# A two-layer diffusion transformer: the total of the softmax sums formed between two key products, two scalings put later, the first loads on two queues, and the second feed-forward network's first elements placed anew

## The chip, the cores and the metric

The kernel runs on one core of one Trainium2 chip. A core has TensorE (matmuls, with weight loads that overlap them), VectorE, ScalarE, GpSimd and SyncE (which here only issues transfers); ScalarE can issue transfers as well. The metric is the device time of one execution in microseconds, with the median over several runs. Lower is better.

## The reference

Sixteen images of 256 tokens with 256 features go through two blocks. Each block is self-attention, cross-attention to a context of 256 tokens with 192 features, and a feed-forward network; every part starts with a layer norm whose scale and shift come from a conditioning vector. All is float32.

```python
# layer 0: 16 heads of 64, rotary positions, inner width 1024
attn_in = adaln(x, cond, ln1, g1, b1)
x = attn(attn_in, attn_in, sa_wq, sa_wkv, sa_wo, sa_bo) + x
x = attn(adaln(x, cond, ln1, g1, b1), ln(context), ca_wq, ca_wkv, ca_wo, ca_bo) + x
x = gelu(adaln(x, cond, ln2, g2, b2) @ ff_w1 + ff_b1) @ ff_w2 + ff_b2 + x
# layer 1: 16 heads of 16, six modulations from silu(cond) @ Wmod + bmod
x = x + attn(h1 @ Wqkv + bqkv) @ Wos + bos
x = x + attn(h2 @ Wq + bq, context @ Wk + bk, context @ Wv + bv) @ Woc + boc
x = x + gelu(h3 @ W1 + b1) @ W2 + b2
# attn: rope(q), rope(k) in layer 0; softmax(q k^T / sqrt(width of a head)) v
```

## The kernel before, in words

**Order.** The kernel writes out the order of work on every engine by hand: a manual schedule covers TensorE (PE), VectorE (DVE), ScalarE (ACT), GpSimd (POOL) and SyncE (SP), and each engine runs its instructions in the order in which the code issues them. Where a line of the code stands is therefore where its instruction stands in its engine's queue. Transfers that SP issues go out in that order too, and one whose data isn't ready holds back those behind it.

**Phases, jobs, steps.** There are six phases: layer 0's self-attention, cross-attention and feed-forward network (phases 0, 1, 2), and layer 1's (3, 4, 5). A phase has 16 jobs, one for each image `b`. A job of attention has two steps (`s` = 0, 1), a job of a feed-forward network four. A job is called by phase and image: 5_2 is image 2 in the last phase. A loop runs over all steps, and each step ends with `scores(i + 1)`, the 128 score matmuls of the next attention step (L751) with their exponentials on ACT (L764, four of 128x1024 a step). So a step of attention stretches from one scores run to the next; the one that forms the probabilities, the sums and the outputs of one half of the heads also prepares queries, keys and values for what follows. PSUM is eight banks of 512 float32 a partition, placed by number; scores fill all eight, four for each half `u` of the step.

**Layer 0's self-attention.** For a step, `stage_t` (L770, DVE) adds the probabilities over pairs of keys, `stage_turn` (L776) transposes the result in 32x32 blocks, and `stage_reduce` (L783) sums it. When a job's four halves are there, `sum_up` forms the totals with one small product against a constant `fold` (eight short matmuls "banks<-fold,rows", L84), takes the reciprocal (L792), writes it to DRAM (`sums_seen`, L795) and reads it back spread over partitions (`spread`, L798, four transfers). `scale` (L807, POOL) multiplies the raw outputs by it, one call for each of four parts. `keys(then, e, half)` forms the keys of the next step, `rotate` the rotary products m (L613 for queries, L619 for keys, DVE) and their differences and sums qk (L628, POOL), which the next scores read. `layer0_sums` forms the probability-weighted values (L818).

Two products are done by a seven-product scheme in place of eight. For the queries this holds in the steps of images 3 to 15 (`queries_by_seven`), for the values it holds for images 2 to 15 (`by_seven`). Where both hold in the first step of a job, the code sets `seven`: these are the first steps of images 3 to 14, twelve in all. `late` is the job before, whose totals are formed there, and `nxt` the one after, whose values are. In them `value_part` forms the next image's values in seven products (L643 to L660 are its copies and additions); its "join" (L654, DVE) adds bank 4 to a part of v, and frees that bank for the last part.

**The next images.** `moments` (L352 to L358) finds the statistics of x, `prepare_norm` the normalized x (L366) and its blockwise transposition (L376, `blocks`), which goes on through DRAM: SP writes `turned` (L381) and reads `fetched` (L391). From `fetched` come the scaled and shifted transposed inputs hT (L424 and L426 on ACT, L428 on POOL or DVE). Images ahead go through this some steps early.

**The start.** SP issues, in this order, the condition, x of image 0, `rows` (all the vectors, 34 KB), the first half of wk and wq, the rotary table, the two halves of wv, x of images 1 and 2, `fold`, `mask`, the second half of wk and wq, bo, wo, and x of images 3 to 15. ACT issues the two modulation matrices (`mod_a`). PE turns `rows` into columns (L156, copied by L157), forms the modulation (L188, L196), transposes the normalized x of image 0 (L1254) and then makes the first products with hT (L84, from 11.06 us). It does some idle products with the identity (L140) between these.

**Feed-forward networks.** Each has also a seven-product form. From a few input blocks `fold_input` (L936 to L939, DVE) forms combinations of hT, called `inner`; `fold_output_weights` (L1010 to L1013, DVE, four operations of 128x512) does the same for the second matrix. In the last phase, images 0 and 1 pass their steps with ordinary products (`ffn_products`, ACT's L903 reads them) while the weights and the inputs of images 2 and 3 are folded; from there on L969 and L989 (DVE) add up pieces of the seven products. Banks of the ordinary products go round by a counter, `next_bank()`.

```python
    def next_bank():
        turn_of_ffn[0] = (turn_of_ffn[0] + 1) % 8
        return turn_of_ffn[0]
```

Of the kernel before, what the change touches and what calls it, by code (L numbers as in the profile page):

```python
# [10 lines left out]
F32 = mybir.dt.float32  # L11
# [32 lines left out]
def fast(ctx: ExitStack, tc: tile.TileContext, a: dict, out: bass.AP, flag):  # L44
# [99 lines left out]
    def condition():  # L144

        sig = work.tile([NB, D], F32, tag="inv", name="sig")
        nc.scalar.activation(sig, cond, AF.Sigmoid)
        soon = stat.tile([NB, 1], F32, tag="ve", name="soon")
# [126 lines left out]
    def load_layer0_attention(kind, part, between=None):  # L275
# [3 lines left out]
        if part in ("first", "last"):  # L279
            i = ("first", "last").index(part)  # L280
            wk, wq = (wtile([P, 2, 512], f"w{n}{i}", f"w{n}{i}_{kind}") for n in "kq")
            nc.sync.dma_start(out=wk, in_=wkv_src[:, :, halves[i]])
            nc.sync.dma_start(out=wq, in_=chunked(a[f"{kind}_wq"])[:, :, halves[i]])
            w[f"wk{i}"], w[f"wq{i}"] = wk, wq
            if between is not None and i == 0:
                between()
# [74 lines left out]
    def normalized(src, found, width, name):  # L361

        mv, rstd = found
        xh = work.tile([P, NT, width], F32, tag="xh", name=f"xh_{name}", bufs=1)
# [798 lines left out]
    def count_outside():  # L1163
# [9 lines left out]
        {"layer": 0, "kind": "attn", "cross": False, "load": lambda part: load_layer0_attention("sa", part, load_first),  # L1173
# [9 lines left out]

    def load_first():

        nc.sync.dma_start(out=rope, in_=a["rope"])
        load_phase(0, "values")
        for b in range(1, 3):
            load_x(b)
        for dst, name in ((fold, "fold"), (mask, "mask")):  # L1190
            nc.sync.dma_start(out=dst, in_=a[name])
# [43 lines left out]
    phases[0]["make_mod"] = phases[0]["mod_load"]()  # L1235
    load_x(0)
    nc.sync.dma_start(out=rows, in_=a["rows"])
    for part in ("first", "last", "early", "output"):
        load_phase(0, part)
    for b in range(3, NB):  # L1240
        load_x(b)

    silu = condition()
    jobs[0]["hraw"] = banks[:, 6:8, 0:N]
    found = moments(xs[0], "first")
    xh = normalized(xs[0], found, D, "first")  # L1250
    phases[0]["mod"] = phases[0]["make_mod"](3, silu)
    for c in range(KC):
        for t in range(NT):
            nc.tensor.transpose(  # L1254
                jobs[0]["hraw"][:, c, t * P : (t + 1) * P], xh[:, t, c * P : (c + 1) * P], ident
            )
    idle_products(2)
# [14 lines left out]
    for i, (j, s) in enumerate(steps):  # L1272
# [39 lines left out]
        if ffn:  # L1312
# [8 lines left out]
            if b == 0 and s == (1 if layer0 else 0):  # L1321
# [36 lines left out]
            if s == 2:  # L1358
# [5 lines left out]
                if b == 1:  # L1364
                    fold_output_weights(job["phase"], nc.vector)
                    if not layer0:
# [6 lines left out]
            if s == 3:  # L1373
# [23 lines left out]
                elif b == 1:  # L1397
                    fold_input(jobs[j + 1 : j + 3], nc.vector)
                    prepare_moments(fourth)
        elif layer0:  # L1400
# [10 lines left out]
            if queries_by_seven(then):  # L1411
# [3 lines left out]
                stage_t(job, 2 * s)  # L1415
                stage_turn(job, 2 * s)
# [778 lines left out]
```

## Time and profile before

| | |
|---|---|
| median of three runs | 2155.43 us (2154.51 to 2158.4) |
| the profiled execution | 2155.3 us, with a span of 2153.5 us |
| PE busy | 2134.9 us (99%) |
| DVE busy | 1665.5 us (77%) |
| POOL busy | 1338.1 us (62%) |
| ACT busy | 905.2 us (42%) |
| DMA | 117.83 MB, 55 GB/s on average |
| granted clock of PE | 9 of 9 tenths shown, in every slice of the span |

The span runs from the first to the last instruction that the profiler recorded; the execution's own time is 1.8 us longer. Matmuls are pipelined and their ends are modelled, so a busy PE is not a PE at its peak. A group in the timeline shows its start, its busy time, the engine, the line, the output and inputs, how many instructions it holds, and in brackets the idle time before it with what ended it. In the rows of groups the busy time, the mean of one in ns, and the idle time with its releaser follow each other. "DMA a<-b" as a releaser means that the transfer into a had to land.

### The profile page before, as it was taken

The page shows a single profiled execution, that of the slowest core. Times are in us where ns is not written, and L with a number is a line of the kernel's source. Part 1 is how long each engine was busy: PE and PEld are TensorE (multiplying, and loading weights), DVE is VectorE, ACT ScalarE, POOL GpSimd, SP SyncE. Part 2 cuts the span into 40 slices and gives each one's busy share as a digit, 9 for nine tenths or more (in the row PEclk, how much of TensorE's full clock was granted, in tenths as well). Part 3 has the DMA queues.
Part 4 walks back from the last instruction along what each step waited for, and adds up shares of the span by engine and source line. Part 5 has one row for each costly group of instructions (what it writes and reads, how often), then busy time and mean ns, then how long its engine had stood idle before and what let it go on. Part 6 is the DMA issues. An engine that isn't in the chain of part 4 may idle for free.

```text
span 2153.5 us, 112523 instructions
## 1 busy us (share of the span) xinstructions
PE 2134.9 (99%) x51248; PEld 1440.9 (67%) x51248; DVE 1665.5 (77%) x3060; ACT 905.2 (42%) x1455; POOL 1338.1 (62%) x1346
## 2 busy tenths in 40 slices
PE   9999999999999999999999999999999999999998
PEld 5666767766766666666666668887655656566787
DVE  6877887877888988888888777864777777777765
ACT  3333333333333332333323334443666666665442
POOL 4888778778767877686776766672322323235773
PEclk9999999999999999999999999999999999999999
DMA  6111110110133221211212123221221232223321
GB/s 196 30 38 23 28 38 23 29 38 23 32 87 88 76 59 35 60 42 44 59 35 59 26 73 94 54 48 23 63 44 41 48 102 63 57 49 82 75 64 39
DMA packets 307039, 117.83 MB, mean 55 GB/s; under 512 B 243364, under 2 KB 289784, under 8 KB 306424
## 3 DMA queue, kind: packets, MB, share of 16 engines
q1 hardware_dynamic: 306008, 110.02, 20.5%
q8 instruction: 403, 6.60, 1.3%
q14 instruction: 84, 0.69, 0.1%
q10 hardware_dynamic: 544, 0.52, 0.1%
HBM read 77.14 MB, written 33.29 MB: 51 GB/s over the span
## 4 chain that ended last, share of the span: by engine, by line
PE 66%; POOL 2%; DVE 1%; SPq 0%; DMA 0%; issue 0%; ACT 0%; DVEq 0%; POOLq 0%; ACTq 0%
PE banks L84 42%; PE banks L751 11%; PE banks L837 5%; PE banks L818 5%; PE banks L687 1%; PE banks L504 1%; POOL raw L807 1%; POOL qk L716 0%; POOL folded L1100 0%; DMA spread<-sums_seen 0%; DVE x L1054 0%; POOL folded L1023 0%; SPq L381 0%; SPq L391 0%; SPq L798 0%
## 5 line engine op out<-in xcount | busy, mean ns | idle before, releaser
L764 ACT ACTIVATE pr<-banks 128x1024 f32<-128x1024 f32 x576 | 487.3, 937 | 442.9 <-PE banks L751 312.6
L716 POOL TENSOR_TENSOR qk<-m,m 128x512 f32<-128x512 f32 x152 | 222.3, 1484 | 121.4 <-DVE m L708 118.6
L751 PE MATMUL banks<-qk 32*64 32x256 f32 x8192 | 242.1, 378 | 5.2 <-POOL qk L628 4.3
L770 DVE TENSOR_TENSOR both<-pr 128x1024 f32<-128x1024 f32 x128 | 168.9, 1319 | 94.5 <-ACT pr L764 92.7
L818 PE MATMUL banks<-pr,v 128*32 128x256 f32 x4096 | 240.5, 379 | 0.0
L751 PEld LDWEIGHTS banks<-qk 32*64 32x64 f32 x8192 | 183.8, 131 | 68.1 <-POOL qk L628 18.5
L828 ACT COPY raw<-banks 128x512 f32<-128x512 f32 x128 | 75.1, 587 | 331.1 <-PE banks L818 300.4
L708 DVE TENSOR_TENSOR m<-banks,rope 128x512 f32<-128x512 f32 x304 | 189.6, 678 | 18.5 <-POOL qk L716 10.9
L628 POOL TENSOR_TENSOR qk<-m,m 128x256 f32<-128x256 f32 x208 | 166.1, 824 | 57.9 <-DVE m L619 33.0
L818 PEld LDWEIGHTS banks<-pr,v 128*32 128x32 f32 x4096 | 132.4, 110 | 93.5 <-issue 16.8
L807 POOL TENSOR_TENSOR raw<-raw,spread 128x512 f32<-128x512 f32 x128 | 162.3, 1298 | 36.2 <-DMA spread<-sums_seen 34.7
L454 POOL TENSOR_TENSOR x<-x,bo_b 128x256 f32<-128x256 f32 x96 | 73.3, 783 | 163.5 <-DVE xh L366 163.5
L879 POOL TENSOR_TENSOR oT<-oT,spread 128x256 f32<-128x256 f32 x64 | 45.8, 737 | 205.5 <-DVE spread L878 205.5
L776 DVE STREAM_TRANSPOSE squares<-both 128x1024 f32<-128x1024 f32 x128 | 158.7, 1240 | 2.2
L783 DVE TENSOR_REDUCE rows<-squares 128x32 f32<-128x1024 f32 x128 | 155.0, 1211 | 1.3
L1100 POOL TENSOR_TENSOR folded<-raw,raw 128x512 f32<-128x512 f32 x90 | 143.1, 1617 | 2.4
L837 PE MATMUL banks<-pr,wide_v 128*32 128x256 f32 x2048 | 134.3, 379 | 0.0
L84 PE MATMUL banks<-hT,wq_ca 128*32 128x256 f32 x2048 | 133.9, 379 | 0.0
L751 PE MATMUL banks<-q,k 32*64 32x256 f32 x4096 | 127.9, 381 | 0.0
L84 PE MATMUL banks<-hT,wk_sa 128*32 128x256 f32 x2048 | 125.2, 381 | 0.5 <-ACT hT L424 0.5
L1054 DVE TENSOR_TENSOR x<-banks,x 128x256 f32<-128x256 f32 (+2 forms) x150 | 79.6, 531 | 55.4 <-PE banks L84 49.0
L751 PEld LDWEIGHTS banks<-q,k 32*64 32x64 f32 x4096 | 87.5, 131 | 37.7 <-issue 13.6
(270 smaller groups left out, 4392.1 us busy)
## 6 DMA issues: line engine op xcount, KB each, us to landing
turned<-blocks SPq DMA_DIRECT2D x380, 64.0 KB
fetched<-turned SPq DMA_DIRECT2D x380, 64.0 KB
spread<-sums_seen SPq DMA_DIRECT2D x128, 128.0 KB
x<-in_x SPq DMA_DIRECT2D x16, 256.0 KB
fetched_c<-turned_c SPq DMA_DIRECT2D x64, 64.0 KB
cT<-in_ctx_turned SPq DMA_DIRECT2D x16, 256.0 KB
out<-x SPq DMA_DIRECT2D x15, 256.0 KB
ctx<-in_ctx SPq DMA_DIRECT2D x16, 192.0 KB
```

The costliest lines, as they stand in the source:

```text
L84: nc.tensor.matmul(out[cut], lhsT[:, cut], rhs, start=start, stop=stop, **more)
L628: nc.gpsimd.tensor_tensor(out, cos[i], sin[1 - i], (ALU.subtract, ALU.add)[i])
L708: nc.vector.tensor_tensor(m, pq, rope[:, s : s + 1, :].to_broadcast([P, 2, N]), ALU.mult)
L716: nc.gpsimd.tensor_tensor(r, x, y, (ALU.subtract, ALU.add)[out])
L751: nc.tensor.matmul(banks[64 * g : 64 * g + 64, at + h, t * N : (t + 1) * N], lhs, rhs, start=(half == 0 and (t == 0 or job["layer"] == 1)) ...
L764: nc.scalar.activation(pr[:, one], sc[:, one], AF.Exp, scale=0.125 if job["layer"] == 0 else 0.25)
L770: nc.vector.tensor_tensor(both, pr[:, :, 0, :], pr[:, :, 1, :], ALU.add)
L776: nc.vector.transpose(job["squares"].rearrange("p b k -> p (b k)"), job.pop("both").rearrange("p h n -> p (h n)"))
L783: nc.vector.tensor_reduce(job["rows"][:, u, :], job.pop("squares"), AX.X, ALU.add)
L807: nc.gpsimd.tensor_tensor(part, part, spread[:, u : u + 1, :].to_broadcast([P, 2, N]), ALU.mult)
L818: nc.tensor.matmul(o[32 * h : 32 * h + 32, half, :], v[:, t, col : col + 32], pr[:, h, t, :], start=(t == 0), stop=(t == NT - 1),)
L837: nc.tensor.matmul(o[32 * h : 32 * h + 32], v[:, t, 4 * c + h, 32 * e : 32 * e + 32], pr[:, h, t, :], start=(t == 0), stop=(t == NT - 1),)
```

## The change

Nothing is added to what is computed, and no shapes change. Four things are placed differently.

- **Start.** `rows` goes out second on SP, ahead of x of image 0, and `fold` and `mask` follow x. The first half of wk, wq and the rotary table are issued by ACT, between the sigmoid of the condition and the exponential of the condition (`soon`). The normalized x of image 0 lies in a buffer of the weights' pool that wv uses later, and the loads of wv and all behind it stand after the four transposes of that x in the code.
- **The twelve `seven` steps.** The total is formed in bank 3 between the two halves of the first keys, with its reciprocal and transfers there; before, it was formed in bank 5 after the first part of the values. `scale` is called for parts 0 and 1 where it was called for 0, 1 and 2, and for 2 and 3 at the end, where it was called for 3. The "join" stands ahead of the first half of `layer0_sums`.
- **The border to layer 1's feed-forward network.** In the last step of its cross-attention, the normalization of image 2 and the moments of image 3 for the network are issued between the two halves of the sums (they stood after both, and in the next step). The counter of banks is set to 7, so that the first step's own products begin with bank 0.
- **The folding of the second matrix** in layer 1's feed-forward network stands in the last step of image 1, behind `fold_input`, and no longer in the step before.

```diff
@@ -141,10 +141,11 @@
                 bank(0, 2, P), ident, ident.unsqueeze(1).to_broadcast([P, 2, P]), start=True, stop=True
             )
-    def condition():
+    def condition(load):
         sig = work.tile([NB, D], F32, tag="inv", name="sig")
         nc.scalar.activation(sig, cond, AF.Sigmoid)
+        load()
         soon = stat.tile([NB, 1], F32, tag="ve", name="soon")
         nc.scalar.activation(soon, cond[:, 0:1], AF.Exp)
         silu = work.tile([NB, D], F32, tag="inv", name="silu")
@@ -272,18 +273,16 @@
-    def load_layer0_attention(kind, part, between=None):
+    def load_layer0_attention(kind, part, eng=nc.sync):
         halves = [slice(i * 512, (i + 1) * 512) for i in range(4)]
         wkv_src = chunked(a[f"{kind}_wkv"])
         w = {}
         if part in ("first", "last"):
             i = ("first", "last").index(part)
             wk, wq = (wtile([P, 2, 512], f"w{n}{i}", f"w{n}{i}_{kind}") for n in "kq")
-            nc.sync.dma_start(out=wk, in_=wkv_src[:, :, halves[i]])
-            nc.sync.dma_start(out=wq, in_=chunked(a[f"{kind}_wq"])[:, :, halves[i]])
+            eng.dma_start(out=wk, in_=wkv_src[:, :, halves[i]])
+            eng.dma_start(out=wq, in_=chunked(a[f"{kind}_wq"])[:, :, halves[i]])
             w[f"wk{i}"], w[f"wq{i}"] = wk, wq
-            if between is not None and i == 0:
-                between()
         if part == "values":
             w["wv"] = wtile([P, 2, H * 64], "wv", f"wv_{kind}")
             for i in range(2):
@@ -358,10 +357,10 @@
         nc.gpsimd.tensor_tensor(rstd, ve, neg_half, ALU.pow)
         return mv, rstd
-    def normalized(src, found, width, name):
+    def normalized(src, found, width, name, pool=work, tag="xh"):
         mv, rstd = found
-        xh = work.tile([P, NT, width], F32, tag="xh", name=f"xh_{name}", bufs=1)
+        xh = pool.tile([P, NT, width], F32, tag=tag, name=f"xh_{name}", bufs=1)
         for t in range(NT):
             nc.vector.tensor_scalar(
                 xh[:, t, :], src[:, t, :], mv[:, t, 0:1], rstd[:, t : t + 1], ALU.subtract, ALU.mult
@@ -1170,7 +1169,7 @@
     phases = [
-        {"layer": 0, "kind": "attn", "cross": False, "load": lambda part: load_layer0_attention("sa", part, load_first),
+        {"layer": 0, "kind": "attn", "cross": False, "load": lambda part: load_layer0_attention("sa", part, nc.scalar if part == "first" else nc.sync),
          "mod_load": lambda: layer0_modulation(1)},
         {"layer": 0, "kind": "attn", "cross": True, "load": lambda part: load_layer0_attention("ca", part), "mod_load": None},
         {"layer": 0, "kind": "ffn", "cross": False, "mod_load": lambda: layer0_modulation(2),
@@ -1180,15 +1179,6 @@
         {"layer": 1, "kind": "ffn", "cross": False, "mod_load": lambda: layer1_modulation(3),
          "load": lambda part: load_ffn("L1_xcond_W1", "L1_xcond_W2", "L1_xcond_b1", "L1_xcond_b2", "b", part)},
     ]
-    def load_first():
-        nc.sync.dma_start(out=rope, in_=a["rope"])
-        load_phase(0, "values")
-        for b in range(1, 3):
-            load_x(b)
-        for dst, name in ((fold, "fold"), (mask, "mask")):
-            nc.sync.dma_start(out=dst, in_=a[name])
     def load_phase(p, part):
         ph = phases[p]
@@ -1233,27 +1223,33 @@
             stage_rotary(then[0], 2 * then[1] + e, half, 2 * e)
     phases[0]["make_mod"] = phases[0]["mod_load"]()
+    nc.sync.dma_start(out=rows, in_=a["rows"])
     load_x(0)
-    nc.sync.dma_start(out=rows, in_=a["rows"])
-    for part in ("first", "last", "early", "output"):
-        load_phase(0, part)
-    for b in range(3, NB):
-        load_x(b)
-    silu = condition()
+    for dst, name in ((fold, "fold"), (mask, "mask")):
+        nc.sync.dma_start(out=dst, in_=a[name])
+    def load_first():
+        load_phase(0, "first")
+        nc.scalar.dma_start(out=rope, in_=a["rope"])
+    silu = condition(load_first)
     jobs[0]["hraw"] = banks[:, 6:8, 0:N]
     found = moments(xs[0], "first")
-    xh = normalized(xs[0], found, D, "first")
+    xh = normalized(xs[0], found, D, "first", wpool, "wv")
     phases[0]["mod"] = phases[0]["make_mod"](3, silu)
     for c in range(KC):
         for t in range(NT):
             nc.tensor.transpose(
                 jobs[0]["hraw"][:, c, t * P : (t + 1) * P], xh[:, t, c * P : (c + 1) * P], ident
             )
+    load_phase(0, "values")
+    for b in range(1, 3):
+        load_x(b)
+    for part in ("last", "early", "output"):
+        load_phase(0, part)
+    for b in range(3, NB):
+        load_x(b)
     idle_products(2)
     prepare_input(jobs[0])
     for e in range(2):
@@ -1318,7 +1314,9 @@
             fourth = jobs[j + 4] if j + 4 < len(jobs) and b < NB - 1 else None
             if s == 1 and b > 0 and third is not None:
                 prepare_norm(third)
-            if b == 0 and s == (1 if layer0 else 0):
+            if b == 0 and s == 0 and not layer0:
+                turn_of_ffn[0] = 7
+            if b == 0 and s == 1 and layer0:
                 prepare_moments(third)
             if b == 2 and s == 0 and layer0:
                 add = finish(jobs[j - 3], next_bank(), later=True)
@@ -1362,8 +1360,9 @@
                     prepare_norm(third)
                     prepare_fetch(after)
                 if b == 1:
-                    fold_output_weights(job["phase"], nc.vector)
-                    if not layer0:
+                    if layer0:
+                        fold_output_weights(job["phase"], nc.vector)
+                    else:
                         show_sums(jobs[j - 2])
                         for one in jobs[j + 1 : j + 3]:
                             prepare_input(one, nc.scalar)
@@ -1396,6 +1395,8 @@
                     scale(prev)
                 elif b == 1:
                     fold_input(jobs[j + 1 : j + 3], nc.vector)
+                    if not layer0:
+                        fold_output_weights(job["phase"], nc.vector)
                     prepare_moments(fourth)
         elif layer0:
             then = attention(i + 1, 0)
@@ -1413,17 +1414,19 @@
                 if seven:
                     fold_tokens(nxt, nc.gpsimd)
                 stage_t(job, 2 * s)
+                keys(then, 0, 0)
+                if seven:
+                    sum_up(late, 3)
                 stage_turn(job, 2 * s)
-                for half in range(2):
-                    keys(then, 0, half)
+                keys(then, 0, 1)
                 rotate(then, 0, 1)
                 query_part(then, 0)
                 if s == 1:
                     fold_inner(late, nc.gpsimd, 7, 6)
                 if seven:
                     value_part(nxt, 0)
-                if s == 0:
-                    sum_up(late, 5 if seven else 6)
+                elif s == 0:
+                    sum_up(late, 6)
                 if make_mod:
                     make_mod["mod"] = make_mod["make_mod"](6)
                 for half in range(2):
@@ -1433,7 +1436,7 @@
                 stage_reduce(job, 2 * s)
                 if seven:
                     rotate(then, 1, 1)
-                    scale(late, 0, 1, 2)
+                    scale(late, 0, 1)
                     value_part(nxt, 1)
                     query_part(then, 2)
                     query_part(then, 3)
@@ -1441,17 +1444,17 @@
                     value_part(nxt, "first")
                     query_part(then, 4)
                     value_part(nxt, 2)
+                    value_part(nxt, "join")
                     layer0_sums(job, 0, 5, (0,))
                     query_part(then, 5)
                     rotate(then, 0, 0)
                     query_part(then, 6)
                     rotate(then, 1, 0)
                     layer0_sums(job, 0, 5, (1,))
-                    value_part(nxt, "join")
                     value_part(nxt, 3)
                     layer0_sums(job, 1, 6)
                     value_part(nxt, 4)
-                    scale(late, 3)
+                    scale(late, 2, 3)
                 else:
                     query_part(then, 2)
                     layer0_sums(job, 2 * s, 4)
@@ -1551,8 +1554,12 @@
                 stage_a(then[0], then[1], at)
             if nxt["kind"] == "ffn" and s == 1:
                 ffn_products(nxt, 0, at)
+            border = nxt["kind"] == "ffn" and s == 1
             for e in range(2):
                 layer1_sums(job, s, e, at + 2 + e)
+                if border and e == 0:
+                    prepare_norm(third)
+                    prepare_moments(jobs[j + 4])
                 if s == 1:
                     finish(prev, at + 1, (e,))
                 elif nxt["kind"] == "attn":
@@ -1564,7 +1571,8 @@
             if s == 0:
                 prepare_moments(third)
             else:
-                prepare_norm(third)
+                if not border:
+                    prepare_norm(third)
                 prepare_input(after)
                 if job["cross"] and job["b"] == 5:
                     fold_input_weights(phases[job["p"] + 1], nc.gpsimd)
```

## The prediction

> **What bounds the kernel now.** I read the page first: busy rows, then the chain of waits.
>
> ```profile
> PE 2134.9 (99%) x51248; PEld 1440.9 (67%) x51248; DVE 1665.5 (77%) x3060; ACT 905.2 (42%) x1455; POOL 1338.1 (62%) x1346
> ...
> PE 66%; POOL 2%; DVE 1%; SPq 0%; DMA 0%; issue 0%; ACT 0%; DVEq 0%; POOLq 0%; ACTq 0%
> ...
> L751 PE MATMUL banks<-qk 32*64 32x256 f32 x8192 | 242.1, 378 | 5.2 <-POOL qk L628 4.3
> ...
> L751 PEld LDWEIGHTS banks<-qk 32*64 32x64 f32 x8192 | 183.8, 131 | 68.1 <-POOL qk L628 18.5
> ...
> L807 POOL TENSOR_TENSOR raw<-raw,spread 128x512 f32<-128x512 f32 x128 | 162.3, 1298 | 36.2 <-DMA spread<-sums_seen 34.7
> ```
>
> TensorE is busy 99% and holds the chain, so work moved on VectorE, GpSimd or a queue pays only where TensorE waits for it. The last three rows name one such wait: layer 0's self scores (L751) wait for the rotated pair (L628, GpSimd), and GpSimd waits for the spread reciprocals (L807). The page doesn't say in which steps; the timeline does. From one scores run to the next, the steps that form the next image's values by seven products take 19.93 us at their best (starts 182.58, 222.36, 262.15) and 20.31 to 21.10 at worst. Here is the worst, 585.92 to 607.02:
>
> ```profile
> 594.27 0.36 DVE L792 RECIPROCAL inv<-banks 128x32 f32<-128x32 f32 x1 [0.64 <-ACT banks L643]
> ...
> 602.51 3.77 POOL L807 TENSOR_TENSOR raw<-raw,spread 128x512 f32<-128x512 f32 x3 [2.92 <-DMA spread<-sums_seen]
> ...
> 604.85 0.16 PEld L84 LDWEIGHTS banks<-sums_of_weights,hT 128*32 128x32 f32 x8 [0.39 <-DVE v L654]
> ...
> 606.23 2.11 POOL L628 TENSOR_TENSOR qk<-m,m 128x256 f32<-128x256 f32 x3
> ...
> 607.02 1.35 PE L751 MATMUL banks<-qk 32*64 32x256 f32 x28 [1.10 <-POOL qk L628]
> ```
>
> GpSimd idles 2.92 us until the spread lands, does three scalings (3.77), and only then the rotary pairs which the scores need: TensorE waits 1.10. The 0.39 is a second wait: the fifth value product waits for the join (L654), queued behind four rotary operations.
>
> **Seven steps** (twelve: images 3 to 14, first half). The total's matmul moves between the two first key products, the reciprocal ahead of the turn (L776) and the rotaries, two of four scalings go behind the rotary pairs, the join ahead of L613. No operation is added.
>
> Stalls at the end of these steps, beyond the steady 0.28 us of TensorE between two scores runs, read step by step: 0.55, 0.39, 0.55, 0.61, 0.01, 0.90, 0.65, 1.17, none in three others: 4.83 us. The eight steps behind them take 20.11 us in place of 19.85, where the scores' second half waits 0.206 for the last pair: 1.65. Together 6.48. (The twelfth step, from 141.85, waits 0.73 for the folded tokens, L532, which the change leaves.)
>
> What becomes of them, in the clean step from 262.15: TensorE reaches the total at 265.79 plus half of 1.93, 266.75. VectorE ends L770 at 267.40, so the reciprocal runs there, and no longer at 270.50: 3.1 us earlier. The spread, whose wait ended at 277.07, is there at about 274, when GpSimd has just begun a rotary pair (274.40 to 275.83). Then two scalings, 2 x 1.26, to 278.4; the rotary pairs, which could start when VectorE's products are there (278.7 and 280.4), end at 281.8, before 282.08. Two scalings follow (2.6 us) ahead of L1100, which took 4.83 from 284.92 after a scaling that ended at 284.85; they now end at about 284.7, so nothing behind them is late. Seven of the eight stalls go. In the worst step SP holds the reciprocal: four issues of turned_c (591.04 to 594.91) and ctx (to 595.57) precede it, so its transfer leaves at 595.67 as before; only the scaling order helps, 1.3 of GpSimd time against a stall of 1.4, and 0.3 remains. So -6.2. The join now fits VectorE's idle 1.68 us ahead of L613 (601.18); the wait it causes is of size 0.1 (TensorE) in the clean steps, twelve times: -1.2. Sum -7.4. Bounds: -8 if the worst step is cured too; -5 if two more stalls of 0.6 stay, and half of the second waits and joins (1.2 + 0.8 + 0.6 less).
>
> The new wait: the total's bank is one that the second Exp (L764) of the step reads. Four take 3.77 from 264.20, so the second ends at 266.09, 0.66 ahead of TensorE. Counted at nothing under that cover.
>
> **The start.** TensorE's first product of x waits for this chain:
>
> ```profile
> 1.65 0.41 SPq L1237 DMA_DIRECT2D rows<-in_rows  x1
> ...
> 5.30 0.37 PE L156 MATMUL banks<-ident,rows 68*128 68x68 f32 x1 [0.98 <-DMA rows<-in_rows]
> ...
> 11.06 1.07 PE L84 MATMUL banks<-hT,wk_sa 128*32 128x256 f32 x16 [0.53 <-ACT hT L424]
> ```
>
> rows goes out second, not third. TensorE's idle products end at 4.31, so its transpose runs 0.98 earlier at best; x's load goes out 0.46 later, and the statistics (L352, 5.85, with x landed at 4.86) gain 0.5 to 1.0. The first product comes at about 10.0 to 10.5. wk, wq and rope move to ScalarE's queue behind its sigmoid (3.00, 0.42): issued at about 3.45 rather than 2.10, wk has 6.5 us to land where it took 7.15 (landed 9.25) among the same bytes; wq is needed 0.67 later. They hold ScalarE's table load (3.44) by 1.3 us; its next work is at 8.56, so that is covered. Against it: wv's load now waits for the transposes of x (L1254, 9.05 to 9.67; the tile shares its buffer) and leaves at about 8.9, not 3.55, with x1 to x15 behind it. The loads run at some 380 GB/s (8 to 28 us), so the stream's end moves by 0 to 0.8; at its end stands image 1's turned input, whose hT (L424, 37.15) is done 0.9 before TensorE needs it at 38.78. Kept gain 1.08 at best, lost 0.3 at worst. I take -0.5.
>
> The Trainium skill, "DMA: Bandwidth & Descriptors", section "Issuing engines are not separate DMA queues", speaks against the second queue: transfers from all engines run on the same 16 DMA engines, and several issuers save only issue time. By it the gain would be SyncE's three issues (0.39 + 0.47 + 0.47 = 1.33 us). The trace of before can't decide it: ScalarE's queue carried only two loads there (4.5% of the 16 engines' first 40 us, against 74.9% for SyncE's). My -0.5 rests on rows' place alone, not on the queue.
>
> **Border of the second FFN** (layer 1's). Two waits: 0.32 us at 1948.87 for L856, which goes, because the first bank is now a free one, and this, two images on:
>
> ```profile
> 1965.81 1.93 PE L84 MATMUL banks<-inner,input_w_L_xcond_b 128*32 128x256 f32 x32 [2.06 <-DVE inner L937]
> ```
>
> Moving norm and moments ahead of the second half's sums makes the second next image's turned block ready about 1.75 us earlier (1954.22 before), so hT (1964.17) and inner (L936) come 1.2 to 2.2 earlier: up to 2.06 is to be had. But the four output folds (L1010 to L1013, 1961.83 to 1964.44, 2.6 us), which ran while VectorE waited, now stand between inner and the six (L969), as do the moments (1.1). TensorE needs the six for its bank: it ended at 1968.11 and the product ran at 1968.42. Now it ends 5.4 us after inner's third operation, at 1968.0 to 1969.0. What the first wait gives, this takes: net with the 0.32 from -0.4 to +0.6; I take +0.2. The ends are -2.4 (both waits go) and +0.8.
>
> **Sum**: -7.4 - 0.5 + 0.2 = -7.7 on the profiled execution's 2155.3 (span 2153.5, 1.8 around it; the median of three, 2155.43, is the same to 0.1): 2147.6. Behind these places TensorE idles about 1% in all, so there is no slack in which a gain could vanish: what is saved stays saved.
>
> **Rivals.**
> 1. The stalls are only partly cured (SP's issues hold the reciprocal in more steps, or VectorE's displaced rotaries make L628 late in turn): half of part two, -3.7, start 0 and border +0.6: -3.1, 2152.2. For it: the worst step, and that L619 now runs 0.4 us later. Against: 1.9 us of GpSimd idle stand ahead of 274.40. This is no change by the bound below.
> 2. Slower: the total between the keys waits for an exponential. If ScalarE's Exp that frees its bank were the step's fourth (ends 267.97), TensorE would stand 1.2 us plus 0.1 of start-up in each of 12 steps: +15.6, in all +7.9, 2163.2. It turns to a loss from 1.3 us of delay on the second Exp (0.66 of cover, and 7.7/12). For it: the total moves from an idle bank to one just read. Against: ScalarE waits 7.82 for the scores, so it starts at once.
> 3. The start gains nothing, and wv's late load pushes the stream by its whole 5.4 us delay less the 0.9 of cover: +4.5 in place of -0.5, in all -2.7, 2152.6. Against: the queues are full from 8 us on, so the 5 us are not left empty.
>
> **Chances.** Sum 0.80, rival 1 0.09, rival 3 0.04, rival 2 0.04, something else on the slower side 0.03. A measurement of this kernel tells about 0.2% (4.3 us) from no change: faster means below 2151.1. The sum's own ends are -8 - 1.1 - 2.4 = -11.5 and -5 + 0.3 + 0.8 = -3.9; the extremes don't fall together, so 2144.8 below, and 2152.0 above, which takes in most of rival 1. Faster 0.81, same 0.12, slower 0.07.
>
> **What would show it.** Right: the reciprocal ahead of L776, some 5.3 us into a seven step; L807 in pairs, the second behind L628; L751's wait for L628 down from 4.3 and 18.5 us to under 2 and 13; all seven steps at 19.9 us; the first product at 10.0 to 10.5; at 1965 a shorter wait for inner and a new one of the next product for L969. Wrong: a wait of L84 for L764 ahead of the total, seven steps still above 20.3, or hT of image 1 after 38.8.

## The result, and the profile after

The changed kernel took 2148.69 us (median of seven runs, 2147.22 to 2152.08) against 2155.99 (2154.51 to 2158.4) for the kernel before: ratio 0.9966, with a 95% interval from 0.9955 to 0.9978, or 7.3 us less. A second set, in a later round, gave 2147.74 and a ratio of 0.9965 (0.9951 to 0.9979). The profiled execution of after (2152.08, span 2150.3) was the slowest of its seven, so its trace shows only 3.2 of the 7.3 us; the experiments below say which of its waits come back in other runs.

First the same rows of the page of after (lines moved up by one: L750 scores, L627 rotary pairs, L806 scaling), and one row of its list of waits (total, times, longest):

```profile
PE 2136.8 (99%) x51248; PEld 1442.3 (67%) x51248; DVE 1676.3 (78%) x3060; ACT 905.9 (42%) x1455; POOL 1340.8 (62%) x1346
...
L750 PE MATMUL banks<-qk 32*64 32x256 f32 x8192 | 240.9, 378 | 1.0 <-POOL qk L715 0.5
...
L806 POOL TENSOR_TENSOR raw<-raw,spread 128x512 f32<-128x512 f32 x128 | 162.1, 1296 | 22.9 <-DMA spread<-sums_seen 22.5
```

```profile
PEld banks L750 <- POOL qk L627: 10.6, 13, 0.9
```

The scores' idle time fell from 5.2 to 1.0 us, and the weight loads' wait for the rotary pairs from 18.5 to 10.6. The clean step, which began at 262.15 and took 19.93 us, now reads so in the timeline:

```profile
266.48 0.24 PE L84 MATMUL banks<-fold,rows 128*32 128x32 f32 x8
...
267.12 0.35 DVE L791 RECIPROCAL inv<-banks 128x32 f32<-128x32 f32 x1
...
267.50 0.34 SPq L794 DMA_DIRECT2D sums_seen<-inv  x1
...
270.78 1.75 SPq L797 DMA_DIRECT2D spread<-sums_seen  x4
...
275.37 2.53 POOL L806 TENSOR_TENSOR raw<-raw,spread 128x512 f32<-128x512 f32 x2 [0.48 <-DMA spread<-sums_seen]
...
276.47 0.69 DVE L653 TENSOR_TENSOR v<-banks,v 128x512 f32<-128x512 f32 x1 [1.50 <-ACT v L651]
...
278.58 1.43 POOL L627 TENSOR_TENSOR qk<-m,m 128x256 f32<-128x256 f32 x2 [0.68 <-DVE m L612]
```

It began at 261.95. The total has no wait, the reciprocal is 5.2 us into the step (8.35 before), and GpSimd, which came late to the rotary products before, now waits for them (0.68). The join stands in VectorE's idle time. Of the 3.2 us by which the reciprocal is earlier, half is lost again on the way: the read of the spread went out 3.3 us behind the write of `sums_seen` (267.50 to 270.78), 1.5 us before the change (270.89 to 272.37), and the scalings start 13.4 us into the step, where it was 14.9.

Two other places of this trace lost time. At the border, in the timeline:

```profile
1958.47 1.93 PE L84 MATMUL banks<-inner,input_w_L_xcond_b 128*32 128x256 f32 x32 [0.52 <-DVE inner L936]
...
1962.61 0.69 DVE L968 TENSOR_TENSOR sums<-banks,sums 128x512 f32<-128x512 f32 x1
...
1963.35 1.07 PE L84 MATMUL banks<-inner,input_w_L_xcond_b 128*32 128x256 f32 x16 [2.09 <-DVE sums L968]
...
1964.24 3.37 PE L84 MATMUL banks<-w_b,g 128*32 128x128 f32 x64
```

Inner's wait fell from 2.06 to 0.52, and a new one of 2.09 came for "the six" (L968, VectorE's sum of product six and a copy of product one), which now stands behind the output folds. The last line is the same 64 matmuls that took 1.93 us at full pace in other profiles. The table by stretches says why (the third number from the end is the granted clock, then DMA share and GB/s):

```profile
1960.00:1964.00 4.00, 1.91 (x36) 0.94 (x32) 3.69 (x11) 0.84 (x2) 0.70 (x1) 1.00 0.34 75
1964.00:1966.00 2.00, 2.00 (x48) 1.89 (x44) 1.97 (x5) 1.10 (x2) 1.93 (x3) 0.63 0.90 295
1966.00:1968.00 2.00, 2.00 (x40) 1.79 (x36) 0.30 (x1) 0.91 (x2) 1.92 (x2) 0.51 1.04 299
```

TensorE was busy 1.91 of 4 us, and then ran some 3.4 us at half clock: 1.6 us lost.

The start, in the timeline of after:

```profile
4.10 0.32 PE L157 MATMUL banks<-ident,rows 68*128 68x68 f32 x1
...
9.12 1.91 PE L140 MATMUL banks<-ident 128*128 128x256 f32 x4
9.34 0.56 ACT L423 ACTIVATE hT<-banks,add_a,fac_a 128x256 f32<-128x256 f32 x1 [1.76 <-PE banks L1243]
...
10.96 1.61 PE L84 MATMUL banks<-hT,wk_sa 128*32 128x256 f32 x16
...
38.73 0.60 ACT L423 ACTIVATE hT<-fetched,add_a,fac_a 128x256 f32<-128x256 f32 x1 [7.50 <-DMA fetched<-turned]
```

rows' transpose is 1.2 us earlier and hT 1.1 (9.34 in place of 10.44), but the first product only 0.1: the four idle matmuls ahead of it took 1.91 us where they took 1.03 before. They run in order, so the product waited for them and not for hT, which was ready at 9.90. The first scores are at 25.41 (24.97 before). And hT of image 1 comes 1.6 us later than the 37.15 of before.

### The profile page after: what moved, and what is told of

Read it like the earlier page. It is cut to its first block, busy times and chain, and to the rows that moved or that the text cites. A ratio compares the mean times of both kernels' runs of the same rounds, so it can differ in the third digit from the quotient of the medians.

```text
span 2150.3 us, 112524 instructions
## 1 busy us (share of the span) xinstructions
PE 2136.8 (99%) x51248; PEld 1442.3 (67%) x51248; DVE 1676.3 (78%) x3060; ACT 905.9 (42%) x1455; POOL 1340.8 (62%) x1346
## 4 chain that ended last, share of the span: by engine, by line
PE 85%; DVE 3%; POOL 3%; issue 1%; DMA 1%; SPq 0%; ACT 0%; DVEq 0%; POOLq 0%; ACTq 0%
PE banks L84 54%; PE banks L750 15%; PE banks L817 9%; PE banks L836 5%; PE banks L686 2%; PE banks L503 1%; POOL raw L806 1%; POOL folded L1099 1%; POOL qk L627 0%; DMA spread<-sums_seen 0%; POOL qk L715 0%; DVE x L1053 0%; DVE bn L351 0%; POOL rstd L357 0%; SPq L797 0%
## 5 line engine op out<-in xcount | busy, mean ns | idle before, releaser
L769 DVE TENSOR_TENSOR both<-pr 128x1024 f32<-128x1024 f32 x128 | 177.8, 1389 | 86.1 <-ACT pr L763 84.6
L750 PE MATMUL banks<-qk 32*64 32x256 f32 x8192 | 240.9, 378 | 1.0 <-POOL qk L715 0.5
L750 PEld LDWEIGHTS banks<-qk 32*64 32x64 f32 x8192 | 184.7, 131 | 61.3 <-issue 16.8
L707 DVE TENSOR_TENSOR m<-banks,rope 128x512 f32<-128x512 f32 x304 | 189.7, 679 | 22.5 <-POOL qk L715 13.4
L627 POOL TENSOR_TENSOR qk<-m,m 128x256 f32<-128x256 f32 x208 | 168.0, 832 | 61.9 <-DVE m L618 38.6
L806 POOL TENSOR_TENSOR raw<-raw,spread 128x512 f32<-128x512 f32 x128 | 162.1, 1296 | 22.9 <-DMA spread<-sums_seen 22.5
L1099 POOL TENSOR_TENSOR folded<-raw,raw 128x512 f32<-128x512 f32 x90 | 141.5, 1600 | 2.4
L84 PE MATMUL banks<-hT,wq_ca 128*32 128x256 f32 x2048 | 134.0, 379 | 0.0
L750 PE MATMUL banks<-q,k 32*64 32x256 f32 x4096 | 128.2, 381 | 0.0
L84 PE MATMUL banks<-hT,wk_sa 128*32 128x256 f32 x2048 | 126.5, 382 | 0.0
L750 PEld LDWEIGHTS banks<-q,k 32*64 32x64 f32 x4096 | 87.4, 131 | 38.0 <-issue 13.9
```

The lines of the kernel that those rows point to most:

```text
L84: nc.tensor.matmul(out[cut], lhsT[:, cut], rhs, start=start, stop=stop, **more)
L627: nc.gpsimd.tensor_tensor(out, cos[i], sin[1 - i], (ALU.subtract, ALU.add)[i])
L707: nc.vector.tensor_tensor(m, pq, rope[:, s : s + 1, :].to_broadcast([P, 2, N]), ALU.mult)
L750: nc.tensor.matmul(banks[64 * g : 64 * g + 64, at + h, t * N : (t + 1) * N], lhs, rhs, start=(half == 0 and (t == 0 or job["layer"] == 1)) ...
L769: nc.vector.tensor_tensor(both, pr[:, :, 0, :], pr[:, :, 1, :], ALU.add)
L806: nc.gpsimd.tensor_tensor(part, part, spread[:, u : u + 1, :].to_broadcast([P, 2, N]), ALU.mult)
```

## The experiments

Each kernel's profile gives the same four stretches of TensorE's time: to the first scores; the first six steps; the 24 steps of images 3 to 14 (the seven steps and the ones behind them); and the last, from the start of layer 1's last attention scores to the end of TensorE's last matmul. The middle two are sums of the intervals between scores runs.

| kernel | first scores at | six steps | 24 steps | last stretch |
|---|---|---|---|---|
| before | 24.97 | 116.88 | 485.28 | 206.42 |
| after | 25.41 | 116.67 | 477.20 | 208.51 |
| seven steps alone | 26.13 | 116.27 | 476.85 | 207.93 |
| start alone | 27.22 | 116.05 | 484.63 | 206.42 |
| border alone | 25.00 | 116.32 | 483.13 | 206.25 |
| total alone | 24.82 | 115.88 | 479.59 | 207.77 |
| scale alone | 25.05 | 116.46 | 480.03 | 207.86 |
| join alone | 24.82 | 116.22 | 485.50 | 207.59 |
| total behind the fourth Exp | 23.63 | 117.54 | 492.52 | 206.23 |
| rows second alone | 24.24 | 115.90 | 483.85 | 207.25 |
| folds on GpSimd | 25.19 | 117.39 | 476.84 | 205.06 |
| folds ahead | 24.66 | 117.01 | 477.88 | 204.52 |
| folds ahead, less idle | 25.19 | 116.75 | 476.85 | 204.10 |
| changed again | 25.79 | 116.69 | 476.85 | 207.42 |

What is not in the table (the cross-attention, the first feed-forward network, layer 1's attention) differs by up to 2 us a part between any two profiles, without order that was found; that is of the size of the spread between runs.

**Part by part.** The seven-step edits alone:

```diff
+                keys(then, 0, 0)
+                if seven:
+                    sum_up(late, 3)
...
-                    scale(late, 0, 1, 2)
+                    scale(late, 0, 1)
...
+                    value_part(nxt, "join")
                     layer0_sums(job, 0, 5, (0,))
...
-                    scale(late, 3)
+                    scale(late, 2, 3)
```

> The kernel before with the edits of the twelve seven steps alone (total between the keys, two scalings behind the rotary pairs, the join early). Theory: this part is the whole gain; in the profile after these steps and the ones behind them became 8.0 us shorter in sum, so 8.0 us less than before, ratio 0.9963, steps of 19.81 and 19.85 us. Rival (the gain comes from several parts alike): 4 us or less.

2148.01 us against 2152.93 for before on this chip: 0.9979 (0.997 to 0.9988), 4.9 us less (2.6 to 6.5), where 8.0 were expected. The steps are as expected (19.81 and 19.85, but 20.68 in image 3's, which waits for the folded tokens), and 2148.01 is no slower than the whole change (2148.69), so it is before that was faster here: 2152.93, where the first set had 2155.99. Part of that may be in the steps: unchanged, the 24 took 483.1 to 485.3 us in four profiles, while those with the whole edit took 476.84 or 476.85 in four of six (477.88 at most). What the edit removes is a wait for GpSimd, which itself waits until the spread has landed. That leaves a part open: there is no profile of before on this chip, and from the lowest of these to the changed steps it is still 6.3 us, at the upper end of the interval.

The start alone (rows second, wk, wq and rope on ScalarE's queue, wv behind the transposes):

> The kernel before with the start's edits alone. Theory: hT of image 0 is ready 1.1 us earlier (9.9 in place of 11.0 us), but what TensorE makes of it depends on when its matmuls go from the slow pace (0.43 us for 128x256) to the fast one (0.21): in the profile before that was at 9.0 us, in that after at 12.1, and there the gain was lost (+0.44 us at the first scores). Time within -1.1 and +0.5 us of before, and the pace changes at another moment than in either profile, if it follows no work of the kernel. Rival (the late load of wv and the x stream decide): hT of image 1 late and +1 us or more.

2152.75, ratio 1.0 (0.9991 to 1.0009). In its profile the matmuls went to the fast pace only at 14.9 us, and the first scores came at 27.22 (24.97 before); hT of image 1 came at 39.94. The time shows neither gain nor loss.

The border alone (norm and moments between the sums, counter, folds behind inner):

> The kernel before with the second FFN's border alone (norm and moments between the sums, counter of banks, output folds after inner). Theory: the wait for inner shrinks from 2.06 to about 0.5 us, the wait for L856 (0.32) goes, and a new one of some 2.1 us for the six (L969), which stands behind the folds, takes it back: +0.4 us. If TensorE's pace halves behind that wait as in the profile after (4.5 us at 0.43 us a matmul group of eight 128x128 in place of 0.22), +2.1 us. Rival (the earlier inner pays): -1.5 us.

2151.81, ratio 0.9998 (0.9989 to 1.0007). The two waits went and one of 1.7 us for the six came; the clock stayed at 1.00, and the last stretch is 206.25 where before has 206.42. Neither sign can be told from nothing.

**Which edit of the seven steps counts.**

```diff
# total alone
+                if seven:
+                    sum_up(late, 3)
...
-                if s == 0:
-                    sum_up(late, 5 if seven else 6)
+                elif s == 0:
+                    sum_up(late, 6)
# scale alone
-                    scale(late, 0, 1, 2)
+                    scale(late, 0, 1)
...
-                    scale(late, 3)
+                    scale(late, 2, 3)
# join alone
+                    value_part(nxt, "join")
                     layer0_sums(job, 0, 5, (0,))
...
-                    value_part(nxt, "join")
                     value_part(nxt, 3)
```

> The kernel before, with only the total moved between the two key products (three scalings ahead of the rotary pairs, join behind L613, as before). Theory: with the spread there 3 us earlier, GpSimd's three scalings (3.8 us) end at 17.5 us of the step in place of 18.7 or later, and the rotary pairs are in time in all twelve steps except perhaps the last but three (SP's ctx load holds the reciprocal there): seven steps at 19.93 us, the ones behind them at 19.85; 5 to 6 us less than before in the trace. Rival (both edits are needed): steps above 20.1 remain.

> The kernel before, with only the third scaling moved behind the rotary pairs. Theory: the stalls are 0.4 to 1.2 us, and the pairs come 1.3 us earlier, so this alone removes them too: steps at 19.93 and 19.85 us, 5 to 6 us less than before in the trace, and the two edits are alternatives and not terms that add. Rival (they add): steps of 20.2 or more remain, and half the gain.

> The kernel before, with only the join ahead of L613. Theory: 0.12 us in each of the steps whose end doesn't wait for the rotary pairs, nothing in those where it does: 0.3 to 1.4 us less, within the measurement's spread; the 0.39 us of weight loads behind L654 in the steps go. Rival (L613 is 0.7 us later, and the rotary pairs with it): stalls of 0.7 us more in each, 5 to 8 us longer.

Against 2153.82 of before: total alone 2150.88 (0.999, 0.9981 to 0.9999), scale alone 2150.0 (0.9985, 0.9976 to 0.9994), join alone 2153.32 (0.9999, 0.999 to 1.0008). Total and scale are alternatives: 479.59 and 480.03 us in the 24 steps, with nine steps of 19.93 each, and both together add mainly the last case (the total alone also has one step of 20.13). That is the step in which SP holds the reciprocal (585.92 of before). Here it is in the timelines of the total alone and of the scale alone:

```profile
595.67 3.77 POOL L807 TENSOR_TENSOR raw<-raw,spread 128x512 f32<-128x512 f32 x3 [3.33 <-DMA spread<-sums_seen]
...
600.18 1.16 PE L751 MATMUL banks<-qk 32*64 32x256 f32 x24 [0.79 <-POOL qk L628]
```

```profile
598.18 2.51 POOL L807 TENSOR_TENSOR raw<-raw,spread 128x512 f32<-128x512 f32 x2 [4.27 <-DMA spread<-sums_seen]
...
601.43 0.69 PE L751 MATMUL banks<-qk 32*64 32x256 f32 x16 [1.33 <-POOL qk L628]
```

Alone, either leaves 0.8 to 1.3 us (steps of 20.79 and 21.33); together it takes 19.81 to 19.93. The join alone brings its 0.12 (19.81 for 19.93) only in steps that don't wait for the pairs, three here; with the other two edits it brings it in eleven of twelve (all but image 3's) in four of six profiles.

**The price of the slower rival.** The total in a bank that the fourth exponential reads:

```diff
-                    sum_up(late, 3)
+                    sum_up(late, 7)
```

> The changed kernel, with the total in bank 7, which the step's fourth exponential reads, in place of bank 3, which the second reads. Prices the wait of the slower rival. Theory: TensorE stands 1.2 to 1.3 us at the total in each of twelve steps: steps of 21.0 to 21.1 us, 15 us more than the changed kernel, about 2163. Rival (the wait is caught up later in the step): less than 5 us more.

In this kernel the total's matmul writes into a bank to which value products add, so part of the values isn't the reference's; the instructions are the same in number and size. Its timeline, in a step that began at 264.30:

```profile
266.36 3.77 ACT L763 ACTIVATE pr<-banks 128x1024 f32<-128x1024 f32 x4 [7.82 <-PE banks L750]
...
270.18 0.27 PE L84 MATMUL banks<-fold,rows 128*32 128x32 f32 x8 [1.17 <-ACT pr L763]
```

All twelve steps took 21.19 us, in eleven of them 1.38 more than the 19.81 of the change; image 3's, which waits for the folded tokens anyway, gave 0.5. The 24 steps took 492.52 us, 15.7 more than 476.85, and the kernel 2160.81 us, slower than before (1.0035, 1.0022 to 1.0048). The wait is not caught up.

**rows alone.**

```diff
+    nc.sync.dma_start(out=rows, in_=a["rows"])
     load_x(0)
-    nc.sync.dma_start(out=rows, in_=a["rows"])
```

> The kernel before, with only the load of rows ahead of image 0's x on SyncE; wk, wq, rope and wv stay where they were. Theory (the prediction's: the start's gain rests on rows' place alone): the columns are there 1 us earlier and the first product at 10.0 to 10.5 us in place of 10.9 to 11.1, as with the whole edit; first scores 0.5 to 1.1 us earlier where the matmuls go to their fast pace by 9.5 us, nothing gained where they do so at 11.8 or later. Rival (wk, wq on the same queue behind x hold it): first product still at 10.9 or later, waiting for wk or for x.

The time can't tell it (2154.65, ratio 1.0, 0.9991 to 1.0009), the profile can: first product at 10.33, first scores at 24.24, the sixth step over at 140.14 us. Six profiles with the old start have 140.70 to 142.40 there, six with the whole new one (the one with less idle work left out) 141.17 to 143.27. In this one profile the part of the edit that leaves wv and the queues alone is better than the whole.

**The border mended.** First the folds on GpSimd in image 1's third step, then on VectorE ahead of the addition that waits for TensorE. The edit of the second:

```diff
+                    fold_output_weights(job["phase"], nc.vector)
                     finish(jobs[j - 2], next_bank())
...
-                    if not layer0:
-                        fold_output_weights(job["phase"], nc.vector)
```

> The changed kernel, but the four output folds of layer 1 run on GpSimd in image 1's third step (where VectorE had them before), so that neither inner nor the six stands behind them. GpSimd idles 9.5 us there. Theory: the wait for the six (2.1 us) goes, 0.5 for inner stays, and no slow stretch follows: 2.3 to 3.8 us less than the changed kernel's profiled execution, some 2.5 less than its median, about 2146. Rival (the six waits for its own product, or the folds are late for the output products): as the changed kernel, within 0.5.

> The changed kernel, with layer 1's four output folds on VectorE ahead of the addition that waits for the output product (L1143 of before), where VectorE idled 2.7 us in the changed kernel. Theory: neither inner nor the six stands behind them, and they don't run beside GpSimd (where inner took 0.64 and 1.31 us in place of 0.43): waits of some 0.5 us at the border in place of 3.0, the granted clock stays at 1.00 there; 2 to 3 us less than the changed kernel, 4.6 if that has the slow stretch. Rival (inner waits for its transfer anyway): waits above 1.5 us.

On GpSimd: 2146.4 where before had 2152.93 (0.9973, 0.9964 to 0.9982); the wait for the six is gone, one of 0.94 for inner stays. Ahead on VectorE: 2146.98 where before had 2154.89 (0.9955, 0.9942 to 0.9969), and no wait of TensorE over 0.25 us is left at the border:

```profile
1956.62 0.42 DVE L936 TENSOR_TENSOR inner<-hT,inner 128x256 f32<-128x256 f32 x1
...
1957.22 1.91 PE L84 MATMUL banks<-inner,input_w_L_xcond_b 128*32 128x256 f32 x32
...
1959.81 1.05 PE L84 MATMUL banks<-inner,input_w_L_xcond_b 128*32 128x256 f32 x16
```

The last stretch is 204.5 us (205.06 with the folds on GpSimd) in place of 206.2 to 208.5 with the folds behind inner. In the time this hardly shows: against before, the ratios 0.9973 and 0.9955 lie on both sides of the changed kernel's 0.9966 and 0.9965, and ahead on VectorE it is 0.8 us less than the changed kernel in the same round (2146.98 and 2147.74), where 2 to 3 were expected. **Less idle work** besides:

```diff
-    idle_products(2)
+    idle_products(1)
     prepare_input(jobs[0])
```

> As the kernel with the folds ahead, with one call of two idle matmuls in place of two calls ahead of the first product. Theory: where the matmuls are at the slow pace then, the idle ones end at 10.2 and not 11.0 us, and the first product comes 0.7 us earlier; where they are at the fast pace nothing changes. 0 to 0.7 us less. Rival (the idle matmuls bring the fast pace): it comes 1 us later or more, and 0.5 us are lost.

> The changed kernel once more, on the same chip as the others. Theory: seven steps of 19.81 and 19.85 us again, while the time of the start (first scores between 23.6 and 25.5 us) and of the last stretch (206 to 208.5 us, by whether the granted clock falls behind the wait for the six) differ from the first profile, because both hang on the clock; 5 to 7 us less than before.

2144.38 us (0.9949, 0.9935 to 0.9962) against 2147.74 for the changed kernel on the same chip, five runs of each and without overlap (2143.57 to 2146.55 and 2147.01 to 2148.81): the fastest version here. In both profiles the matmuls were slow until after 12 us, with hT ready at 9.89 and 9.98; the first product came at 10.18 with two idle matmuls ahead of it and at 11.04 with four. That part is read from two profiles only. The changed kernel again had all its seven steps at 19.81 but image 3's, no slow stretch at the border, and a last stretch of 207.42.

## Why the prediction was right, point by point

Forecast 7.7 us less, measured 7.3, within the range. In the profiles two of the three terms were within 0.4 us or so, and one came out with the wrong sign. The times of the parts alone are less kind: 4.9 us (2.6 to 6.5) for the seven steps where 7.4 were forecast, and nothing that can be told from zero for the start and the border. So that the sum is within 0.4 us is in part luck.

- **Seven steps, -7.4 forecast.** The four profiles with these steps unchanged have 484.2 us on average for the 24 steps, the changed ones 476.85 at their usual: -7.4, and -8.1 between the first two traces. Most of the working shows in the trace: the reciprocal 3.2 us earlier, the pairs done at 281.7 with the scalings behind them, 0.12 a step for the join, the weight loads' wait for the pairs below 13 us. Three sizes were off. The spread was there 1.5 us earlier in the step and not 3, because its write took longer to land; GpSimd idled 0.48 us for it, without harm to the pairs, for whose products it then waited 0.68. The steps behind gave 0.26 us each and not 0.206 (20.11 to 19.85). And the worst step, for which 0.3 was to remain, came to 19.90, 0.1 above the others. The working took total and scaling as one sum; the runs show that either alone removes most of it (-4.6 and -4.2 against that average), and that they add only where SP is late.
- **The cover of the total.** Counted at 0.66 us; no wait was seen. The rival's price was 15.6 us, 1.3 in each of twelve steps; measured 15.7, as 1.38 in eleven and 0.5 in image 3's. The wait itself was 1.17 (1.2 forecast), and a step grew by 0.2 more, where 0.1 of start-up was counted.
- **Border, +0.2 forecast.** Inner's wait to 0.5, L856's gone, a new wait for the six of 2.1 us: as foreseen. The last stretch with the edit (206.25, 206.23, 207.42, 208.51) is 207.1 on average, without it (seven profiles) 207.3, so that neither sign is shown. What the prediction had not is the half clock that can follow the longer wait: +1.6 in one profile of four.
- **Start, -0.5 forecast.** In the profiles this term failed in two steps; the time of the start alone (ratio 1.0, 0.9991 to 1.0009) can't tell 0.5 us. The step "the first product comes at about 10.0 to 10.5" did not hold: it came at 9.72 in one of six profiles and at 10.75 to 11.87 in the others. hT began at 9.1 to 9.4 us in four of the six, as early as said (in two at 10.1, where x landed late), but the idle matmuls at the slow pace, which stand between hT and the product, were not counted. And "the stream's end moves by 0 to 0.8" was mis-sized: hT of image 1 came at 37.8 to 39.9 us in place of 34.7 to 37.7 (2.1 later on average), and the first of the six steps took up to 0.84 more where TensorE was early. hT after 38.8, named as a sign that the forecast is wrong, was there in three of the six. At the end of the sixth step the edit stands at 142.2 us on average (six profiles) against 141.5: +0.7, with ranges that overlap. rows' place alone, on which the term was said to rest, gave 140.14 in its one profile.

What carried the forecast is the large term, and that was read step by step from waits that TensorE itself had, and not from the work moved.

## What to carry to other kernels

Where one engine is 99% busy, look for the waits that only it has, step by step, and move whatever ends them: here one small matmul and two multiplications, with no work saved. When two edits both shorten the same chain, price them together, not as a sum. An operation that ran while its engine waited is not free to move: find another idle stretch for it (the output folds, 2.6 us, were free ahead of a wait of VectorE and cost 2.1 behind it).

## What the runs showed of the hardware that was not expected

- **TensorE's pace at the start.** The same four idle matmuls of 128x256 took 1.91 us in one profile and 1.03 in another. The change to the fast pace came 6.6 to 9.0 us into the span in eight profiles and at 11.7 to 14.8 in six. Here it is in the changed kernel once more, and in the kernel with the total behind the fourth Exp, which has the same start:

```profile
11.04 1.92 PE L84 MATMUL banks<-hT,wk_sa 128*32 128x256 f32 x16
12.74 1.07 PE L84 MATMUL banks<-hT,wq_sa 128*32 128x256 f32 x16
```

```profile
9.72 1.07 PE L84 MATMUL banks<-hT,wk_sa 128*32 128x256 f32 x16
```

  At the fast pace, and with x there early, the new start does bring the forecast (first scores 23.63, 1.3 us less than before); this is one profile. The column of the granted clock reads 1.00 in all of these stretches, but a trace keeps the clock as a list of records, and there is none yet here: the first, at full rate, begins at the moments given above (8.5 us in the kernel before, 12.1 in the changed one), where the durations change too. Of seven profiles with the old order of wv and wk six change early, of seven with the new one two; whether that is chance or the order's doing stays open.
- **The clock behind a wait.** In the middle of the run the granted clock does show it: 1.00 up to 1964.4, 0.50 from 1964.8 to 1967.6, 1.00 from 1968.0. The Trainium skill, "TensorE: Matmul & The Clock Gate", section 'Part 1: The HAM clock gate (the "warmup" mystery)', has the clock at half or full rate by how busy TensorE was in a free-running window of 3.4 us. The length and the half agree with this trace: its list has 1952.42 us at full rate, then 3.41 at half, then 180.91 at full, and in all fourteen profiles each full-rate record is a whole multiple of 3.413 us long (572 and 53 times here). Counted in such stretches from the first record, the wait of 2.09 us lies whole in the one from 1961.13 to 1964.54, behind which the clock was halved; in the changed kernel again a wait of 2.09 falls on two (0.90 and 1.19 us), and the clock stayed at 1.00. In no other stretch of the fourteen profiles, up to the last 10 us, was TensorE idle for over 1.85 us, and the clock fell nowhere else. Three waits of 2.19 to 2.30 us for inner, in profiles with the old border, fall on two stretches each and halved nothing. So here it was where the wait lay against these stretches that counted, and not its length alone.
- **VectorE beside GpSimd.** inner's first two operations took 0.64 and 1.31 us on VectorE while GpSimd ran the output folds, and 0.43 and 0.42 with the folds ahead on VectorE.
- **A wait without a releaser.** In seven of the fourteen profiles TensorE stands 0.4 to 1.5 us at the same place of the last stretch, among the output products of layer 1's first pair, where the trace names nothing that it waits for. It makes up most of the difference between 206.4 and 207.9 in the last column. The packets of the queue that carries instructions (on the page of after "q8 instruction: 403, 6.60, 1.3%": 403 packets, 6.60 MB, some 64 bytes for each of TensorE's 102496 matmuls and weight loads) give a hint. In just these seven profiles a packet starts between 0.9 us before and 0.1 us after the first of these products (the group banks<-output_w_L_xcond_b,folded, L84), and TensorE goes on 2.3 to 2.5 us after the packet's start; in the seven others it starts 1.3 to 2.3 us after that product. This fits a TensorE that waits for its next instructions; no experiment tested it.
